# Two graph-attention layers and a binarised layer on one core: signs turned through DRAM, column maxima by halves, and work moved at the borders

## The chip, the core and the metric

The kernel runs on one core of a Trainium2 chip. The metric is the device time of one launch in microseconds, the median of several runs. Before the change it is 2627.36 us (three runs, 2627.24 to 2629.74). The engines' names are short here: PE is TensorE (PEld its weight loads), DVE is VectorE, ACT is ScalarE, POOL is GpSimd, SP is SyncE. SP issues nearly all loads, POOL most stores.

## The reference

```python
N, D = 3327, 512                       # x: N x D, adj: N x N of zeros and ones
def gat_layer(x, W, adj):              # W: D x 2D, twice (L = 2), with W_stack[0], W_stack[1]
    Wh, Ws = split(x @ W, 2, axis=-1)
    a = softmax(Wh @ Ws.T, axis=-1) * adj
    return leaky_relu(a @ Wh + x, 0.01)
h = layernorm(x + gat_layer(gat_layer(x, W[0], adj), W[1], adj))
xw = maximum(sign(h), 0) @ sign(weight).T
return layernorm(h + relu(adj @ xw))
```

All is float32 at the interface. The attention is dense, N x N scores for each of two layers; the last step multiplies adj by a matrix that comes from the signs of h.

## The kernel before, in words

**Tiles.** The N rows make NT = 26 tiles of P = 128 (the last one has 127 rows), 13 pairs of tiles (NQ = 13, a pair is called g on the query side, q on the key side) and 7 chunks of four tiles (NC = 7, the last one has two). Products of two-by-two blocks are made with seven multiplications instead of eight; the sums and differences of blocks that this needs are made by DVE, POOL or ACT, or ahead of time in DRAM (`xs_d`, `ws_d`, `gs_d`).

**Stages.** For each layer l, `project` (L297) turns x, makes the values `wh` and their block sums, the keys' block sums (`xs_d`) and the projected queries (`gs_d`). Then `attention` (L549) walks through 13 x 13 steps (g, q). After both layers, adj times xw is accumulated by `aggregate` (L1099), and `finale` (L1114) adds, normalises and writes out.

**A step of attention.** The loop over v (L985) writes out by hand what each step holds. `scores` for a later (chunk c, q, half s) run LOOK = 30 steps ahead of `values` of step v. In between, for steps v + 3 and v + 2: `shift` (L734, subtract the column's maximum), `exponential` (L738, ACT), `running` (L741, the running total), `masked` (L749, times adj), then `sums` (L785) on POOL, which builds the block sums `as` that PE's values product needs. Each piece of work carries a place within the step (0 to 1); the pieces of a step are sorted by it and put on their engines' queues in that order. An engine works through its queue in order. So the places decide what on DVE stands ahead of what. `halved_sums` (0.6), `halved` (0.61) and `exact` (0.62) make 8-bit block sums of adj for the last product, on DVE and ACT; `keep_blocks` stores them from POOL's queue one step later.

**Borders.** In the last step of a chunk's scores, `column_max` (L666) is put into the next step for both pairs of the chunk at once: fold the two rows of maxima (-0.04), turn and reduce and join the four partition groups (0.36), and turn back to `off` (0.9). The first maximum of a chunk is a copy (L648), the first total of a pair as well (L745). In a pair's last step, `take_out` (L827) reads the four accumulator banks of PSUM at 0.34, 0.63, 0.91 and 1.06; the next pair's products write into the same four banks.

**The end of a pair.** `finish` (L853) gives a list of small jobs (`later`), one for each following step, at place 0.7: `norm` (two PE transposes of the totals), `residual(i)` for both tiles (DVE, then a store by POOL), and in the second layer `sign(i)` (mean and comparison, DVE), `turn(i)` (L901: four PE transposes of 128 x 128 bf16 and one ACT copy) and `linear(i)` (four PE products with the sign of weight, then a store of xw or, for the last two pairs, a copy into its place in SBUF). There are 11 jobs for a pair in the second layer, and 9 for the last pair.

**Between the layers.** In the last steps of layer 0, `early` holds loads of the next weights, `turn_w` (DVE), `product_m` (PE, L281) and block sums. Then layer 1's `project` loads the first chunk of x1, transposes it by PE (L329 to L333, 16 transposes of f32, four ACT copies), and DVE makes the first two key sums (`left_sums`, L203).

Of the kernel before, what the change touches and what calls it, by code (L numbers as in the profile page):

```python
# [19 lines left out]
P = 128  # L20
# [10 lines left out]
def kernel(  # L31
# [18 lines left out]
    def rows(t):  # L50
        return min(P, N - t * P)
# [50 lines left out]
    h_d = tc.dram_tile([N, D], F32, name="h_d")  # L102
    xw_d = tc.dram_tile([NT, P, D], F16, name="xw_d")
# [122 lines left out]
    w_rows, w_laid, wT, m_of, wsum_of = {}, {}, {}, {}, {}  # L226
# [7 lines left out]
    def transpose_w(l, h, k, lane):  # L234
        pool, tag = lane
        pt = pool.tile([P, D], F32, tag=tag, name=f"pwT_{l}_{h}_{k}")
        for d in range(KD):
            nc.tensor.transpose(pt[:, ts(d, P)], w_rows[l, h, d][:, ts(k, P)], ident)
        wT[l, h, k] = slot([P, D], F32, f"wTs_{l}_{h}_{k}")
        copy_out(1 if h == 0 else k, wT[l, h, k], pt)  # L240
# [56 lines left out]
    def project(l, pre):  # L297
# [18 lines left out]
        def transpose_first(lane):  # L316

            pool, tag = lane
            xTs[0] = pre.tile([P, KD, CW], F32, tag="xT", bufs=2, name=f"xT_{l}_0")
            pts = [pool.tile([P, CW], F32, tag=tag, name=f"pxt_{l}_{k}") for k in range(KD)]  # L320
            xts = [t.rearrange("r (p k) -> r k p", k=KD) for t in rows_of[0]]
            if l == 0:

                for a in range(CT):
                    for k in range(KD):
                        nc.tensor.transpose(pts[k][:, ts(a, P)], xts[a][:, k], ident)
                for k in range(KD):
                    copy_out(k, xTs[0][:, k], pts[k])
                return  # L329
            for k in range(KD):  # L330
                for a in range(CT):
                    nc.tensor.transpose(pts[k][:, ts(a, P)], xts[a][:, k], ident)
                nc.scalar.copy(xTs[0][:, k], pts[k])  # L333

        def transpose_x(c, a):
            if a == 0:
                xTs[c] = pre.tile([P, KD, CW], F32, tag="xT", bufs=2, name=f"xT_{l}_{c}")
            nc.vector.transpose(
                xTs[c][:, :, ts(a, P)].rearrange("p k (r v) -> p r k v", v=B),
                rows_of[c][a].rearrange("p r (u k) -> p r k u", u=B),  # L340
            )


        load_x(0)
# [8 lines left out]
        transpose_first(acc_lane)  # L353
# [17 lines left out]
        def keys(c, a, between=lambda: None):  # L371

            q = c * CT // 2 + a
            xT = xTs[c]
            j1, j2 = ts(2 * a, P), ts(2 * a + 1, P)
            s12 = slot([P, 2, 2, P], F32, f"s12_{l}_{q}")
            s34 = slot([P, 2, 2, P], F32, f"s34_{l}_{q}")
            of = {
                A11: xT[:, 0:2, j1], A12: xT[:, 2:4, j1], A21: xT[:, 0:2, j2],
                A22: xT[:, 2:4, j2], S1: s12[:, 0], S2: s12[:, 1], S3: s34[:, 0],  # L380
                S4: s34[:, 1],
            }
            left_sums(
                *(of[i] for i in (A11, A12, A21, A22, S1, S2, S3, S4)), between=between
            )
            to = xs_d[l][q]
            for raw in (A11, A12, A21, A22):
                nc.gpsimd.dma_start(out=to[:, raw], in_=of[raw])
            nc.gpsimd.dma_start(out=to[:, S1 : S2 + 1], in_=s12)
            nc.gpsimd.dma_start(out=to[:, S3 : S4 + 1], in_=s34)  # L390
            return of
# [157 lines left out]
    def attention(l, att):  # L549
# [6 lines left out]
        asum, ws, out_ = {}, {}, {}  # L556
# [28 lines left out]
        def scores(c, q, s):  # L585
# [53 lines left out]
            def maximum(i):  # L639
                t = sc[i, q]  # L640
                if q == NQ - 1 and pad:
                    nc.vector.tensor_scalar(
                        t[:, 1], t[:, 1], there[:, 0:1], there[:, 1:2], ALU.mult, ALU.add
                    )
                if q == 0:
                    top[i] = att.tile([P, 2, HW], F32, tag=f"top{i % 2}", bufs=1,
                                      name=f"top_{l}_{i}")
                    nc.vector.tensor_copy(top[i], t)  # L648
                else:
                    nc.vector.tensor_tensor(top[i], top[i], t, ALU.max)  # L650

            if s == 1:

                after.append((-0.05, lambda: maximum(mine[0])))
                if q == NQ - 1:
                    after.extend(column_max(c))
# [9 lines left out]
        def column_max(c):  # L666

            mine = halves_of(c)
            n = len(mine) * HW // B


            part = small.tile([P, CW // B], F32, tag="mxq", bufs=1, name=f"mxq_{l}_{c}")
            quad = small.tile([P, P // B, CW // B], F32, tag="mx4", bufs=1,
                              name=f"mx4_{l}_{c}")
            whole = small.tile([P, CW // B], F32, tag="mx", bufs=1, name=f"mx_{l}_{c}")

            def fold():
                for g in mine:
                    nc.vector.tensor_tensor(
                        top[g][:, 0], top[g][:, 0], top[g][:, 1], ALU.max  # L680
                    )

            def across():
                w = HW // B
                for i, g in enumerate(mine):
                    nc.vector.transpose(top[g][:, 1], top[g][:, 0])
                    nc.vector.reduce_max(
                        part[:, ts(i, w)],
                        top[g][:, 1].rearrange("p (r u) -> p r u", u=B), axis=AX.X,
                    )  # L690
                for a in range(P // B):
                    nc.vector.tensor_copy(quad[:B, a, :n], part[ts(a, B), :n])
                nc.vector.reduce_max(
                    whole[:B, :n], quad[:B, :, :n].rearrange("p a r -> p r a"), axis=AX.X
                )
                for a in range(1, P // B):
                    nc.vector.tensor_copy(whole[ts(a, B), :n], whole[:B, :n])

            def back():
                w = HW // B  # L700
                for i, g in enumerate(mine):
                    off[g] = att.tile([P, 1, HW], F32, tag=f"off{i}", bufs=1,
                                      name=f"off_{l}_{g}")
                    nc.vector.transpose(
                        off[g][:, 0].rearrange("p (r u) -> p r u", u=B),
                        whole[:, ts(i, w)].unsqueeze(2).to_broadcast([P, w, B]),
                    )

            return [(-0.04, fold), (0.36, across), (0.9, back)]
# [28 lines left out]
        def exponential(g, q):  # L738
            nc.scalar.activation(sc[g, q], sc[g, q], AF.Exp)  # L739

        def running(g, q):  # L741

            if q == 0:
                total[g] = att.tile([P, 2, HW], F32, tag="total", name=f"total_{l}_{g}")
                nc.vector.tensor_copy(total[g], sc[g, q])  # L745
            else:
                nc.vector.tensor_tensor(total[g], total[g], sc[g, q], ALU.add)  # L747
# [53 lines left out]
        def values(g, q):  # L801
# [21 lines left out]
            if q == NQ - 1:  # L823
                got += [((i + 1.4) / 7, lambda i=i: take_out(g, i)) for i in (1, 3, 5, 6)]
# [28 lines left out]
        def finish(g):  # L853
# [37 lines left out]
            def sign(i):  # L891
# [7 lines left out]
                nc.vector.tensor_scalar(ba[:r], hh[:r], mv[:r, t, 0:1], None, ALU.is_gt)  # L899

            def turn(i):  # L901
                r = rows(mine[i])
                pt = ps_tr.tile([P, KD, P], BF16, tag="tr", name=f"pbt_{mine[i]}")
                for k in range(KD):
                    nc.tensor.transpose(pt[:, k, :r], held[i][:r, ts(k, P)], ident_h[:r, :r])
                held[i] = att.tile([P, KD, P], BF16, tag="baT", bufs=1, name=f"baT_{mine[i]}")
                nc.scalar.copy(held[i][:, :, :r], pt[:, :, :r])
# [18 lines left out]
            if not last:  # L926
                return [norm, lambda: residual(0), lambda: fetch(1), lambda: None,
                        lambda: residual(1)]
            free = [] if g == NQ - 1 else [lambda: None]
            return [  # L930
                norm, lambda: residual(0), lambda: (sign(0), fetch(1)), *free,
# [4 lines left out]
        if last:  # L936

            early, wts = {}, {}

            def load_weight(k):  # L940
                wts[k] = ring.tile([P, D], F32, tag="h", name=f"wT_{k}")
                nc.sync.dma_start(out=wts[k], in_=weightT[ts(k, P), :])
# [4 lines left out]
        else:  # L947

            end = len(ahead) - LOOK
            early, parts = {}, []  # L950
# [13 lines left out]
            n = len(steps) - end - 2  # L964
            early[end + 2] = [(0.2, begin_m)]
            for i, do in enumerate(product_m(l + 1, ch_lane)):
                early.setdefault(end + 2 + i * n // (KD * KD), []).append(
                    (0.3 + 0.4 * (i % 2), do)
                )
            early.setdefault(end + 7, []).append((0.6, lambda: parts.extend(sums_w(l + 1))))  # L970
            for i in range(4):
# [89 lines left out]
    def load_products(v):  # L1061
# [11 lines left out]
        for t in range(2 * NQ - 4):  # L1073
            g, i = divmod(t, 2)
            made = (g + 1) * NQ - 1 + (6, 11)[i]
# [38 lines left out]
    def finale(att):  # L1114
# [75 lines left out]

        constants()
        product_sums(NQ - 1)
# [143 lines left out]
```

## Time and profile before

| what | value |
|---|---|
| median of three runs | 2627.36 us |
| the profiled execution, its own time | 2626.88 us |
| its span, first to last instruction | 2625.1 us |
| granted TensorE clock, mean | 0.998 |
| DVE, ACT, POOL busy | 81%, 30%, 42% |
| DMA, mean rate | 243 GB/s |
| start of the first and the last step of attention's values, layer 0 | 279.0 and 1239.3 us |
| the same, layer 1 | 1500.9 and 2477.7 us |

The profile is one execution. Its page gives for each engine the time that it was busy, and groups of instructions by line and shape with the number, the busy time, the mean duration in ns, and the idle time before them with what ended it. The list of waits names an engine's line, what it waited for, the sum in us, how often, and the longest. The timeline lists instructions by start and length; a number in brackets is the idle time before, with the one that ended it. A table of stretches gives, for an engine, how long it was busy in each, with the granted clock and the share of the DMA engines' time. An engine that is named as the releaser may have been done long before; then it was another one.

### The profile page before, as it was taken

The numbers are of one execution on the slowest core, as the hardware profiler recorded it, in microseconds if no ns is written. First come the engines' busy times: TensorE is split into PE (matmuls) and PEld (weight loads), VectorE is DVE, ScalarE is ACT, GpSimd is POOL, SyncE is SP. The second block draws the span as 40 slices with busy tenths as digits, with TensorE's granted clock in tenths as the row PEclk, the third lists the DMA queues.
The fourth block names the chain that finished last, engine by engine and source line by source line (L and its number), as shares of the span: only waits on it lengthen the run. The fifth ranks groups of instructions, "written<-read, shape, count | busy, mean of one in ns | idle before, by whom it ended". The sixth has DMA issues, their size and how long they took to land. (4 is left out here: it accounts for less than half of the span.)

```text
span 2625.1 us, 40169 instructions
## 1 busy us (share of the span) xinstructions
PE 2582.4 (98%) x12552; PEld 2238.6 (85%) x12552; DVE 2116.0 (81%) x4376; ACT 785.9 (30%) x1954; POOL 1104.1 (42%) x2025
## 2 busy tenths in 40 slices
PE   9999999999999999999999999999999999999998
PEld 6888888888888888887888888888888888888787
DVE  6764888899898896777875689989899898767876
ACT  2323332333333332211332333333333333222143
POOL 3640344444444444546562144444444444455510
PEclk9999999999999999999999999999999999999999
DMA  6855777787777776787875668777787776688775
GB/s 209 296 193 180 240 242 269 232 276 249 263 245 246 267 241 223 236 254 245 284 243 179 226 223 283 250 242 265 238 283 245 236 271 233 226 263 264 260 249 171
DMA packets 308055, 639.16 MB, mean 243 GB/s; under 512 B 34855, under 2 KB 175745, under 8 KB 306298
## 3 DMA queue, kind: packets, MB, share of 16 engines
q1 hardware_dynamic: 272140, 530.29, 61.7%
q0 software_dynamic: 35664, 106.18, 11.0%
q8 instruction: 103, 1.69, 0.3%
q14 instruction: 118, 0.97, 0.1%
q10 hardware_dynamic: 30, 0.03, 0.0%
HBM read 529.69 MB, written 106.67 MB: 242 GB/s over the span
## 5 line engine op out<-in xcount | busy, mean ns | idle before, releaser
L580 PE MATMUL pZ<-gs,xs 128*128 128x256 f32 x2496 | 636.8, 379 | 2.0 <-ACT u L597 1.7
L790 POOL TENSOR_TENSOR as<-s 128x128 f32<-128x128 f32 x338 | 163.8, 485 | 1042.9 <-DVE s L752 888.2
L580 PEld LDWEIGHTS pZ<-gs,xs 128*128 128x128 f32 x2496 | 473.2, 190 | 69.2 <-ACT u L597 3.6
L817 PE MATMUL acc<-ws,s 128*128 128x256 f32 x1352 | 402.2, 379 | 0.0
L817 PE MATMUL acc<-wh,s 128*128 128x256 f32 x1352 | 355.7, 379 | 0.6 <-DVE s L752 0.4
L817 PE MATMUL acc<-ws,as 128*128 128x256 f32 x1352 | 348.0, 380 | 7.0 <-issue 4.0
L739 ACT ACTIVATE s<-s 128x512 f32<-128x512 f32 x338 | 213.4, 631 | 428.4 <-DVE s L736 428.3
L580 PE MATMUL pY<-gs,xs 128*128 128x256 f32 x1248 | 320.6, 379 | 1.7 <-ACT p L597 1.7
L817 PEld LDWEIGHTS acc<-ws,as 128*128 128x128 f32 x1352 | 255.9, 190 | 48.8 <-issue 8.9
L817 PEld LDWEIGHTS acc<-wh,s 128*128 128x128 f32 x1352 | 256.7, 190 | 36.2 <-DVE s L752 1.4
L817 PEld LDWEIGHTS acc<-ws,s 128*128 128x128 f32 x1352 | 256.0, 190 | 34.5
L650 DVE TENSOR_TENSOR top<-top,s 128x512 f32<-128x512 f32 x312 | 222.5, 726 | 73.1 <-ACT s L637 53.3
L580 PEld LDWEIGHTS pY<-gs,xs 128*128 128x128 f32 x1248 | 236.8, 190 | 35.0 <-ACT p L597 2.8
L736 DVE TENSOR_TENSOR s<-s,off 128x512 f32<-128x512 f32 x338 | 248.4, 735 | 0.1
L752 DVE TENSOR_TENSOR s<-s,adj 128x512 f32<-128x512 f32 x338 | 238.3, 705 | 8.9
L747 DVE TENSOR_TENSOR total<-total,s 128x512 f32<-128x512 f32 x312 | 232.5, 745 | 0.0
L792 POOL TENSOR_TENSOR as<-s 128x128 f32<-128x128 f32 x338 | 208.6, 617 | 26.5
L597 ACT COPY u<-pZ 128x256 f32<-128x256 f32 x312 | 115.7, 371 | 323.2 <-PE pZ L580 322.6
L817 PE MATMUL acc<-wh,as 128*128 128x256 f32 x676 | 202.5, 381 | 0.0
L791 POOL TENSOR_TENSOR s<-s 128x128 f32<-128x128 f32 x338 | 186.7, 552 | 27.4
L793 POOL TENSOR_TENSOR as<-s,as 128x128 f32<-128x128 f32 x338 | 181.8, 538 | 26.5
L622 DVE TENSOR_TENSOR s<-p,u 128x256 f32<-128x256 f32 x156 | 67.6, 433 | 139.0 <-ACT u L597 137.9
(218 smaller groups left out, 3864.0 us busy)
## 6 DMA issues: line engine op xcount, KB each, us to landing
ws<-ws_d SPq DMA_DIRECT2D x338, 512.0 KB, 3.8
xs<-xs_d SPq DMA_DIRECT2D x182, 512.0 KB, 5.9
adj<-in_adjT_dram SPq DMA_DIRECT2D x324, 256.0 KB, 4.3
xs<-xs_d SPq DMA_DIRECT2D x156, 384.0 KB, 6.4
gs_d<-gsp POOLq DMA_DIRECT2D x88, 256.0 KB, 3.0
gs<-gs_d SPq DMA_DIRECT2D x12, 1792.0 KB, 11.5
adj_d<-ab POOLq DMA_DIRECT2D x169, 112.0 KB, 3.9
ahl<-adj_d SPq DMA_DIRECT2D x78, 224.0 KB, 4.9
```

Source lines behind the costliest of these rows:

```text
L580: nc.tensor.matmul(ch[bank], xs[c, q, a][:, k], gs[c][:, b, k], start=(start and k == 0), stop=(k == 1), skip_group_check=True,)
L597: nc.scalar.copy(ch[name], ch[bank])
L650: nc.vector.tensor_tensor(top[i], top[i], t, ALU.max)
L736: nc.vector.tensor_tensor(s, s, off[g].to_broadcast([P, 2, HW]), ALU.subtract)
L739: nc.scalar.activation(sc[g, q], sc[g, q], AF.Exp)
L747: nc.vector.tensor_tensor(total[g], total[g], sc[g, q], ALU.add)
L752: nc.vector.tensor_tensor(s, s, adj[g, q], ALU.mult)
L790: nc.gpsimd.tensor_tensor(s3, a11, a21, ALU.subtract)
L791: nc.gpsimd.tensor_tensor(a21, a21, a22, ALU.add)
L792: nc.gpsimd.tensor_tensor(s2, a21, a11, ALU.subtract)
L793: nc.gpsimd.tensor_tensor(s4, a12, s2, ALU.subtract)
L817: nc.tensor.matmul(acc[g][i // 2][:, i % 2], a[i], b[i], start=(q == 0 and i % 2 == 0), stop=(q == NQ - 1), skip_group_check=True,)
```

## The change

It changes these things:

- **Signs.** For the first 11 of 13 pairs, the sign tile `ba` is stored to a DRAM tensor `ba_d` by POOL, loaded one step later by SP in four pieces of 32 partitions (`lay`, into the ring buffer that also holds xres and x0), and turned by DVE in blocks of 32 x 32 two steps after that. `fetch(1)` moves behind `turn(0)`. A pair has 13 jobs instead of 11. The last two pairs keep the PE transposes, with columns taken at a stride of four; weightT's rows are read in the matching order. The last but one pair's norm comes one step later.
- **Maxima.** `column_max` takes one pair. The first pair's four jobs (fold, turn, across, back) stand in the step after the chunk's last scores, the second pair's two, two, three and four steps after, at 0.68. The first maximum is taken of q = 0 and q = 1 together, and the copy falls away.
- **Totals.** For q = 0 ACT makes the exponential twice, once into the total; DVE's copy falls away.
- **take_out** of the second accumulator bank goes from 0.63 to 0.59.
- **Between the layers.** Layer 1's first chunk of x1 is loaded in pieces in steps 160 to 163, turned by DVE in steps 165 and 166 into a buffer of the `gs` ring, and its key sums are made in step 167; PE's transposes there fall away. `product_m` starts one step later. The copies of the turned weights in layer 0 are all ACT's.
- **The end.** `product_sums(NQ - 1)` is written ahead of `constants()`.

```diff
+    ba_d = tc.dram_tile([NT, P, D], BF16, name="ba_d")
...
-        copy_out(1 if h == 0 else k, wT[l, h, k], pt)
+        nc.scalar.copy(wT[l, h, k], pt)
...
-        load_x(0)
+        if l == 0:
+            load_x(0)
+        else:
+            xTs[0] = x_first[l]
...
-        transpose_first(acc_lane)
+        if l == 0:
+            transpose_first(acc_lane)
...
+            of = keys_first.pop((l, q), None) or key_sums(l, q, a, xTs[c], between)
...
-                if q == 0:
+                if q == 1:
...
-                    nc.vector.tensor_copy(top[i], t)
-                else:
+                    nc.vector.tensor_tensor(top[i], sc[i, 0], t, ALU.max)
+                elif q > 1:
...
-                    after.extend(column_max(c))
+
+                    after.extend(column_max(mine[0]))
+                    for i in mine[1:]:
+                        for n, (_, do) in zip((2, 2, 3, 4), column_max(i)):
+                            early.setdefault(v + n, []).append((0.68, do))
...
-            return [(-0.04, fold), (0.36, across), (0.9, back)]
+            return [(-0.04, fold), (0.2, turn), (0.5, across), (0.7, back)]
...
-            nc.scalar.activation(sc[g, q], sc[g, q], AF.Exp)
...
+                nc.scalar.activation(total[g], sc[g, q], AF.Exp)
+            nc.scalar.activation(sc[g, q], sc[g, q], AF.Exp)
...
-                nc.vector.tensor_copy(total[g], sc[g, q])
...
-                got += [((i + 1.4) / 7, lambda i=i: take_out(g, i)) for i in (1, 3, 5, 6)]
+                    for i, at in ((1, 0.34), (3, 0.59), (5, 0.91), (6, 1.06))
...
+                if g < NQ - 2:
+                    nc.gpsimd.dma_start(out=ba_d[t], in_=ba)
+
+            def lay(i):
+
+                bt = held[i] = ring.tile([P, P // B, P], BF16, tag="xr", name=f"bt_{mine[i]}")
+                load_laid(nc.sync, bt, ba_d[mine[i]], P)
...
+                    nc.vector.transpose(
+                        held[i].rearrange("p k (r v) -> p r k v", v=B),
+                        bt.rearrange("p r (u k) -> p r k u", u=B),
+                    )
...
+                return [
+                    norm, lambda: residual(0), lambda: sign(0), lambda: lay(0), lambda: None,
+                    lambda: (turn(0), fetch(1)), lambda: linear(0), lambda: residual(1),
+                    lambda: sign(1), lambda: lay(1), lambda: None, lambda: turn(1),
+                    lambda: linear(1),
+                ]
...
-            n = len(steps) - end - 2
+            n = len(steps) - end - 3
...
+                early.setdefault(n - 9 + a, []).append((0.9, lambda a=a: load_first(a)))
+                early.setdefault(n - 4 + a // 2, []).append((0.45, lambda a=a: turn_first(a)))
...
+                early.setdefault(n - 2, []).append((0.6 + a / 10, lambda a=a: keys_of_first(a)))
...
-            made = (g + 1) * NQ - 1 + (6, 11)[i]
+            made = (g + 1) * NQ - 1 + (7, 13)[i]
...
+        product_sums(NQ - 1)
         constants()
-        product_sums(NQ - 1)
```

## The prediction

> **What bounds the kernel now.** I read the page first, then TensorE's (PE's) waits, then the stretches where it waits. Lines are those of the kernel before. All durations are of the one profiled execution: span 2625.1 us, 2626.9 us with what lies around it, 0.5 us under the median of the three runs (2627.4).
>
> ```profile
> PE 2582.4 (98%) x12552; PEld 2238.6 (85%) x12552; DVE 2116.0 (81%) x4376; ACT 785.9 (30%) x1954; POOL 1104.1 (42%) x2025
> ```
>
> PE is busy in 98% of the span, 42.7 us are not. Some 11.8 us of these are the tail after the last matmul (2613.3 us), so only 31 us are gaps. A change can gain in two ways: fewer matmuls, or fewer gaps. The gaps, from PE's waits (us in total, times, longest):
>
> ```profile
> PE acc L817 <- issue: 4.0, 3, 1.7
> ...
> PE pX L580 <- DVE s L628: 3.5, 4, 1.2
> ...
> PE pz L865 <- POOL adj L716: 2.7, 1, 2.7
> PE pZ_wh L401 <- DVE s L205: 2.5, 1, 2.5
> PE pm L289 <- DVE wTs L260: 2.0, 1, 2.0
> PE agg L1109 <- DVE wh L212: 1.8, 1, 1.8
> ```
>
> Four of these are single waits at one place each, and the change moves the very work waited for. "Step" below is one (g, q) of attention, 6.1 us (g0 starts at 279.0, g1 at 358.0 us, 13 steps).
>
> **Signs through DRAM (22 of 26 tiles).** Removed: 22 x 4 PE transposes and 22 ScalarE copies (0.59 us each, ACT is 30% busy: nothing). What a tile's transposes take from PE, in the timeline:
>
> ```profile
> 1608.18 0.39 PE L905 MATMUL pbt<-ident_h,ba 128*128 128x128 bf16 x4
> 1608.41 0.65 PE L817 MATMUL acc<-wh,as 128*128 128x256 f32 x2
> 1608.89 0.59 PE L817 MATMUL acc<-ws,s 128*128 128x256 f32 x2
> ```
>
> The next matmul starts 0.23 us after them, and its pair takes 0.48 us from start to start where a pair takes 0.43: 0.28 us a tile, 22 x 0.28 = **6.2 us**. The Trainium skill speaks against the move ("VectorE: DVE Perf Modes", Rules for kernel authors: transpose 128x128 on TensorE if PSUM will do; The three transpose paths: 390 ns there, 311 ns on VectorE). At 390 ns each the gain would be 34 us; the row shows that transposes overlap, so I take 6.2.
>
> Added per tile: one POOL DMA issue (0.55 us, as its other stores), four SP DMA issues (0.43 us each), one VectorE (DVE) transpose. The nearest row for that:
>
> ```profile
> L338 DVE STREAM_TRANSPOSE xT<-xr 128x512 f32<-128x512 f32 x44 | 47.9, 1096 | 0.0
> ```
>
> Same element count and pattern, so 1.1 us; bf16 might be half (0.5), the skill's 4 x 311 ns would be 1.2. 22 x 1.1 = 24 us of DVE time, on the path only where DVE lags. DVE idles 0.5 to 3 us in most steps of layer 1, but hardly in the five steps after a chunk's border and in the last 15 steps. The turn of a pair's second tile comes now at q 11, two steps after the border, and residual and sign of that tile a step later, next to it. I charge **-1.0 us** (0 to -5: five borders at 1 us each).
>
> The new waits: on SP, the load waits for the store of the signs, and ws, adj and xs loads queue behind it. By its place (0.7 of the step) and its 1.4 us of work the sign ends about 1 us into the next step when DVE lags 3 us (an estimate); POOL's stores land after 4 us (xw_d 4.3), so SP is free before that step ends. The ws buffer it loads next is released only then, and is due two steps (12 us) later against 3.8 us to land: hidden, nothing. On POOL the store of the signs stands behind a step's block sums and ahead of the next step's, which PE needs two steps later: 0.55 us there, hidden. fetch(1) now waits for turn(0): due two steps later, 6 us to land, hidden. On DVE the turn waits for a load issued two steps earlier: hidden. Tile 21 alone falls into steps of 3 us; its risk is in the -5.
>
> **The border between the layers.** Removed: 16 f32 transposes of PE, from 1243.4 to 1245.3 us: **1.9 us**; and the key sums that PE waited for are now made in attention's last steps, where DVE is idle nearly whole steps (3.9 us at q 10 and 11). The wait and what follows:
>
> ```profile
> 1249.00:1251.40 2.40, 0.00 (x0) 1.00 0.68 205
> 1251.40:1254.90 3.50, 3.48 (x9) 0.54 0.96 305
> ```
>
> (stretch, its length, PE busy, granted clock.) After the 2.46 us gap the clock is halved for 3.4 us, so the gap costs 2.46 + 1.7 = **4.2 us**. The skill ("TensorE: Matmul & The Clock Gate", Why this matters for your kernels) asks only for gaps under about 3 us; by it the gap would cost 2.5. The row decides: 4.2 (from 1.5, if DVE, which would then be about 2 us nearer to PE, makes it wait at chunk 1). wa was issued at 1233.6 and takes 5.5 us; PE needs it at 1243.3: hidden. The four more SP issues in each of four 3.9 us steps (1.7 us beside 0.8) fit.
>
> The projection product starts a step later, after its DVE turns: the 2.0 us wait goes: **2.0** (1.0 to 2.0). wT's copies on ACT: the 1.16 us gap at 17.4 us waited for a DVE copy: **0.5** (0 to 1.2).
>
> **Take-outs and maxima.** Where a pair g begins, PE waits for the second accumulator bank to be read:
>
> ```profile
> 598.90 0.69 DVE L650 TENSOR_TENSOR top<-top,s 128x512 f32<-128x512 f32 x1
> 599.50 0.42 DVE L843 TENSOR_TENSOR ou<-acc,op 128x256 f32<-128x256 f32 x1
> 599.96 0.42 DVE L844 TENSOR_TENSOR ou<-acc,ou 128x256 f32<-128x256 f32 x1
> ```
> ```profile
> 600.48 0.89 PE L817 MATMUL acc<-ws,as 128*128 128x256 f32 x3 [1.56 <-issue]
> ```
>
> The profile calls it "issue", but PE starts when L844 has read the bank. At 0.59 this read stands ahead of the block sums (0.6), the exact check and the maximum: some 3 us sooner. Such gaps: 1.56, 1.70, 0.72 (598.9, 917.7, 1987.8 us), in all 4.0; I take **3.0** (1.5 to 4.0), since DVE is then further behind.
>
> The maxima by halves: before, a border costs DVE fold 0.8 + across 3.2 + back 0.8 = 4.7 us in one step, plus 0.8 for two first copies and 0.4 to 0.5 for the total's. After: 0.4 + 0.9 + 1.4 + 0.4 = 3.1 us for each half, 6.1 over four steps, since the small copies (0.16 us) come twice. The sum is the same, only flatter. It should remove the pX gaps (1.2 at 425.4, 0.7 at 745.3), but DVE is busy 39.8 of 41 us from 415 to 456 us, and the following gap (1.2 at 457.8, 0.45 at 777.4) comes when DVE's work and a store behind it are done. So PE arrives earlier and waits longer: **0** (0 to 3). Rows of weightT in another order and xw loads that follow their later stores are the same bytes: nothing. The second exponential costs ACT 26 x 0.63 us, a step ahead of its reader: nothing.
>
> **The end.** product_sums ahead of the constants, which wait 1.3 us for an activation table: **1.8 us** (1.0 to 1.8). Pair 11's norm a step later: the 2.7 us wait goes, but the last steps are DVE's:
>
> ```profile
> 2424.00:2432.00 8.00, 7.69 (x15) 1.00 0.95 314
> 2432.00:2436.00 4.00, 2.44 (x5) 1.00 0.91 335
> 2436.00:2476.00 40.00, 38.44 (x74) 1.00 0.87 301
> ```
>
> (third number: DVE busy.) DVE idles only because it waited for that same product (1.5 us), so only this comes back: **1.5** (0 to 2.7).
>
> **Sum.** 6.2 + 1.9 + 4.2 + 2.0 + 0.5 + 3.0 + 1.8 + 1.5 - 1.0 = 20.1 us. 2626.9 - 20.1 = 2606.8 of the profiled execution, 2607.3 as a median. All ends at their best give 27, at their worst 8 us: 2600 to 2619.
>
> **Rivals.**
> - *Gaps only move* (DVE paces the borders and the end, as it already does at 415 to 456 us): only the removed matmuls (8.1), product_sums (1.8), the product's wait (2.0) and the bare border gap count, 12 to 14 us: 2614. For it: DVE at 96% in these stretches. Against: at the border of the layers DVE is idle.
> - *The profile's gaps go entirely*, the pX and end ones too: 27 us, 2600. For it: flatter DVE work. Against: the same sums.
> - *Slower: SP is held by the signs' round trip.* If the store lands more than 5 us into the step of the load, ws and xs come late and PE stops, 22 times. Gone are 20 us at 0.9 us a tile; at 1.6 us a tile the sum is 35 and the time 2642. For it: DMA engines 70 to 80% busy, ACT already waited 20 us for adj_d stores. Against: two steps' reserve, and PE waits for a DMA only 1.2 us in all of attention.
> - *No change*: this needs half that price, 0.9 us a tile.
>
> **Chances.** Forecast 0.60, gaps move 0.24, all gaps go 0.08, no change 0.04, slower 0.04. 0.2% (5.3 us) is about what a measurement of this kernel can tell: faster 0.92, same 0.04, slower 0.04. The range goes from all gaps gone to a little beyond "gaps move": 2600 to 2618.
>
> **What would show it.** PE matmuls fewer by 104 transposes (their records), PE busy down by 8 to 10 us; no wait of pZ_wh on L205's successor, full clock at the border; no 1.6 us gaps at 599 and 918 us; pm, agg and pz gone from the waits. Wrong: new PE waits on ws or xs DMAs, DVE transposes of bt over 1.5 us, gaps in layer 1's steps 0 to 5 after a border above 5 us in sum, or longer gaps at 458 and in the last 15 steps.

## The result and the profile after

The changed kernel takes 2621.64 us (median of 19 runs, 2617.40 to 2626.44), the kernel before in the same measurement 2627.24 us (19 runs, 2623.97 to 2630.91). The ratio is 0.9979, 95% interval [0.9972, 0.9986]: 5.6 us faster. The prediction said 2607.3 us, 2600 to 2618; the gain is a quarter of it. Its profiled execution has a span of 2619.8 us and a granted clock of 0.998. The page's row of engines:

```profile
PE 2579.2 (98%) x12423; PEld 2232.0 (85%) x12448; DVE 2114.9 (81%) x4444; ACT 786.8 (30%) x1956; POOL 1098.2 (42%) x2047
```

PE has 104 transposes less to do (104 weight loads fewer, 12552 before) and is busy 3.2 us less, where 8 to 10 were foreseen (with three buffers, run 1 below, it is 8.5). The idle times of PE up to its last matmul add up to 30.5 us; they were 31.0 before. So the waits named in the prediction went, and others took their place. PE's waits now (us in total, times, longest):

```profile
PE pY L587 <- ACT p L604: 7.1, 5, 2.0
PE pZ L587 <- ACT u L604: 4.7, 6, 1.3
PE acc L821 <- POOL as L796: 4.7, 7, 1.2
...
PE pX L587 <- DVE s L635: 1.4, 2, 0.7
PE acc L821 <- DVE h L856: 1.3, 2, 0.7
PE pz L872 <- POOL adj L720: 0.9, 1, 0.9
```

pm, agg and pZ_wh are gone from the list, and pz fell from 2.7 to 0.9, as foreseen. The waits of pY and pZ for ScalarE have grown. Before, they were:

```profile
PE pZ L580 <- ACT u L597: 1.7, 2, 1.1
PE pY L580 <- ACT p L597: 1.7, 2, 1.2
```

Steps are counted from 0 in each layer. The start of each step, set beside the same step before, says where time is lost: 5.5 us from step 25 to 30 of layer 0, 4.4 us from step 77 to 82 (the two borders of chunks there). In layer 1 a lead of 3.2 us at step 0 falls to 0.8 us at step 156, although 22 tiles x 0.28 us of transposes came off on the way.

What pY waits for stands in the timeline of ACT and DVE at step 25 of layer 0 (start, length, engine and line; the bracket is the idle time before):

```profile
433.14 0.40 ACT L762 CAST ab<-adj 128x256 fp8e4<-128x256 f32 x1 [3.03 <-DMA adj_d<-ab]
433.14 0.29 DVE L776 TENSOR_TENSOR ab<-adj 128x128 fp8e4<-128x128 f32 x1 [3.02 <-DMA adj_d<-ab]
...
433.65 0.36 ACT L604 COPY p<-pY 128x256 f32<-128x256 f32 x1
```
```profile
434.06 1.13 PE L587 MATMUL pY<-gs,xs 128*128 128x256 f32 x4 [1.48 <-ACT p L604]
```

The halved blocks `ab` of adj have two buffers. ACT and DVE stand 3.0 us until an earlier store of blocks has landed (issued by POOL at 426.8, 6.3 us before) and its buffer is free. Behind the waiting cast, in ACT's queue, is the copy of a score product, and PE needs that bank back. The same happens at step 29 (2.04 us of PE), 77 (1.65) and 81 (1.80); at 29 and 81 the timeline names the store for DVE alone, and ACT's cast starts within 0.05 us of DVE's block sum. The waits of ACT and DVE for this store over the whole kernel, before and after:

```profile
ACT ab L758 <- DMA adj_d<-ab: 20.4, 13, 5.4
...
DVE ab L772 <- DMA adj_d<-ab: 17.3, 14, 4.2
```
```profile
ACT ab L762 <- DMA adj_d<-ab: 34.1, 16, 5.0
...
DVE ab L776 <- DMA adj_d<-ab: 30.2, 16, 3.8
```

The gap of 2.04 us also halves the clock, as the 2.46 us at the layers' border did before (stretch, length, PE busy, clock):

```profile
457.00:460.00 3.00, 2.41 (x11) 1.00 0.94 341
460.00:464.00 4.00, 1.96 (x7) 0.84 0.61 230
464.00:468.00 4.00, 4.00 (x16) 0.73 0.27 66
```

Ahead of the last matmul, each kernel's trace has one such half-clock stretch of 3.41 us: it has only moved from the border of the layers to step 29, at 1.7 us in both places.

The small copies of the maxima are the second sign. Groups by shape, before and after (busy us, mean ns):

```profile
L692 DVE COPY mx<-mxq 32x16 f32<-32x16 f32 x48 | 7.8, 163 | 0.9
L697 DVE COPY mx<-mx 32x16 f32<-32x16 f32 x36 | 6.0, 166 | 0.7
```
```profile
L698 DVE COPY mx<-mxq 32x8 f32<-32x8 f32 x104 | 23.7, 228 | 1.1
L703 DVE COPY mx<-mx 32x8 f32<-32x8 f32 x78 | 17.9, 230 | 1.6
```

They move half as many elements and take 0.23 us instead of 0.16; with the few 32x8 ones of before, 41.6 us instead of 16.1, or 1.8 us more at each of 14 borders. In the changed kernel's trace 110 of these 182 copies run while POOL works on a sum; they take 0.27 us in the mean. The other 72 take 0.16.

### The profile page after: what moved, and what is told of

Its sections match the earlier page's. It is cut to its first block, busy times and chain, and to the rows that moved or that the text cites. A ratio compares the mean times of both kernels' runs of the same rounds, so it can differ in the third digit from the quotient of the medians.

```text
span 2619.8 us, 40057 instructions
## 1 busy us (share of the span) xinstructions
PE 2579.2 (98%) x12423; PEld 2232.0 (85%) x12448; DVE 2114.9 (81%) x4444; ACT 786.8 (30%) x1956; POOL 1098.2 (42%) x2047
## 5 line engine op out<-in xcount | busy, mean ns | idle before, releaser
L794 POOL TENSOR_TENSOR as<-s 128x128 f32<-128x128 f32 x338 | 162.3, 480 | 1013.8 <-DVE s L756 824.2
L657 DVE TENSOR_TENSOR top<-top,s 128x512 f32<-128x512 f32 x286 | 200.1, 712 | 77.5 <-ACT s L644 51.8
L796 POOL TENSOR_TENSOR as<-s 128x128 f32<-128x128 f32 x338 | 199.4, 590 | 26.5
```

What stands on the lines that cost most here:

```text
L794: nc.gpsimd.tensor_tensor(s3, a11, a21, ALU.subtract)
L796: nc.gpsimd.tensor_tensor(s2, a21, a11, ALU.subtract)
```

## The experiments

Three theories for the missing 14 us: **S**, the blocks' store with two buffers, which is worse where DVE and ACT come earlier and find more behind it; **C**, the maxima by halves are simply dearer; **D**, the turns of the signs put DVE behind in layer 1. Times are medians of 4 to 10 runs; the kernel before stood at 2626.8 to 2628.1 us beside them. The intervals of the ratios are about 3.5 us wide to each side for 4 to 6 runs, so a difference of 2 or 3 us between two variants needs the traces beside it. Profiled executions with the same code ahead of attention reach its step 0 at 276.4 to 280.2 us; what a change does to a stage is therefore taken from that stage's first step on.

**1. Three buffers for the blocks.**

```diff
-                [P, 7, P], F8, tag="adj_b", bufs=2, name=f"ab_{l}_{g}_{q}"
+                [P, 7, P], F8, tag="adj_b", bufs=3, name=f"ab_{l}_{g}_{q}"
...
-                held[i] = att.tile([P, KD, P], BF16, tag="baT", bufs=1, name=f"baT_{mine[i]}")
+                held[i] = att.tile([P, KD, P], BF16, tag="ba", bufs=1, name=f"baT_{mine[i]}")
```

> The changed kernel, with three buffers in place of two for the halved adjacency blocks (they wait in SBUF for their store to DRAM), and the turned signs in the same buffer as the signs. Theory S (at the chunk borders of layer 0 VectorE and ScalarE now run into the store of these blocks and stand still for 2.4 to 3.0 us, twice a border, and the four gaps of TensorE at 432.6, 460.1, 755.4 and 783.0 us, 7.0 us together, come from that): 4 to 7 us faster than the changed kernel's 2621.6 us, these gaps under 0.5 us each. Theory C (VectorE has simply more work there, the maxima by halves with their small copies): the wait for the store goes, the gaps stay, within 1.5 us of 2621.6.

Measured: 2609.34 us (0.9933 of before [0.9919, 0.9946]), 12.3 us faster than the changed kernel, more than S asked. The list of waits no longer has adj_d for DVE or ACT, and none of the four gaps is over 0.1 us. In the profiled executions the last matmul comes 15.4 us sooner than in the changed kernel: 2.3 us of it before step 0 of layer 0, 12.5 in layer 0, 0.6 after that. (The second part of the edit touches only the signs of layer 1, so the gain in layer 0 is the third buffer's.) DVE's busy time in the stretch after the first border, in the changed kernel and with three buffers:

```profile
431.00:461.00 30.00, 24.85 (x60) 1.00 0.74 233
```
```profile
431.00:461.00 30.00, 29.32 (x63) 1.00 0.78 251
```

So at the border, where there is most to do, DVE stood still for 5 us of 30; with a third buffer for 0.7. A gap costs more than its length: the steps with these gaps are longer by another 0.27 us each, and the half clock costs 1.7.

**2. Maxima of both halves at once** (`column_max` and its call as before; two buffers).

```diff
-                    after.extend(column_max(mine[0]))
-                    for i in mine[1:]:
-                        for n, (_, do) in zip((2, 2, 3, 4), column_max(i)):
-                            early.setdefault(v + n, []).append((0.68, do))
+                    after.extend(column_max(c))
```

> The changed kernel, with the column maxima again for both halves at once, in the step after the last scores, as in the kernel before (the first maximum and the second exponential stay as changed). Theory C (a pair of halves costs VectorE 6.7 to 7.4 us against 4.7 before, since the small copies come twice and, beside GpSimd's sums, take 0.23 us and not 0.16): 3 to 6 us faster than 2621.6, and layer 1 gains back most of the 8.5 us that went missing there. Theory S: the old gap ahead of pX (1.2 us) returns, and the time is 1 to 4 us longer. The prediction's own reading (the same sum, only flatter) gives 0 to 3 us longer.

Measured: 2611.02 us (0.9938 [0.9924, 0.9951]), 10.6 us faster than the changed kernel. C's sign was right, but not its place: in the profiled executions 9.7 us are gained in layer 0, where PE's gaps fall from 10.8 to 5.2 us, 1.4 are lost between the layers, and 2.4 gained in layer 1, where C had foreseen most of 8.5. DVE still waits 28.2 us for the store. The gaps ahead of pX that the halves were to remove do return (0.93 and 0.75 us in layer 0; 1.71 twice in layer 1, where the kernel before has none) and cost less than the halves.

**3. All signs turned by PE** (`ba_d`, `lay` and the DVE turn left out, steps as before; two buffers).

```diff
-                if g < NQ - 2:
-                    nc.gpsimd.dma_start(out=ba_d[t], in_=ba)
...
-                    norm, lambda: residual(0), lambda: sign(0), lambda: lay(0), lambda: None,
-                    lambda: (turn(0), fetch(1)), lambda: linear(0), lambda: residual(1),
-                    lambda: sign(1), lambda: lay(1), lambda: None, lambda: turn(1),
-                    lambda: linear(1),
...
                 *(free if g == NQ - 2 else []), norm, lambda: residual(0), lambda: (sign(0), fetch(1)), *free,
                 lambda: turn(0), lambda: linear(0), lambda: residual(1), lambda: sign(1), *free,
                 lambda: turn(1), lambda: linear(1),
```

The list that served the last two pairs now serves all.

> The changed kernel, with the signs of all 26 tiles again turned by TensorE and copied by ScalarE, without the round trip through DRAM, at the steps of the kernel before. If the signs' part is worth what its own terms say (6.2 less 1.0 us): 5 us slower than 2621.6, 2626 to 2627. Theory D (the turns and the late steps at the borders push VectorE behind, and TensorE waits in layer 1 for most of what it saved): 0 to 2 us slower. Theory C (layer 1 loses to the maxima, not to the turns): 5 us slower again.

Measured: 2619.46 us (0.9968 [0.9956, 0.998]): 2.2 us *faster* than with the signs through DRAM, though every step with a turn on PE is 0.28 us longer, as worked out. PE's gaps in layer 1 fall from 13.5 to 6.5 us; those at steps 24, 26, 76 and 78 are gone. That is beyond all three expectations; D comes nearest. By the medians alone it is hardly clear of noise, but from the first to the last step of layer 1 the traces give 2.5 us as well.

**4. The small copies ahead of POOL's sums.**

```diff
-            return [(-0.04, fold), (0.2, turn), (0.5, across), (0.7, back)]
+            return [(-0.04, fold), (0.1, turn), (0.36, across), (0.7, back)]
...
-                            early.setdefault(v + n, []).append((0.68, do))
+                            early.setdefault(v + n, []).append((0.36 if n == 3 else 0.68, do))
```

> The changed kernel, with the small copies of the maxima at 0.36 of the step, for both halves, and the turn of the first half at 0.1: ahead of the masking and so ahead of GpSimd's sums. Theory C in its narrow form (what is dear is that the copies run beside GpSimd, 0.23 us mean and up to 0.46, in place of 0.16): the copies fall to about 0.16 us, 1.6 us of VectorE at each chunk border, and the kernel is 2 to 4 us faster than 2621.6. If the place of the copies does not matter, or if they hold up the masking instead: within 1.5 us.

Measured: 2618.51 us (0.9969 [0.9956, 0.9981]), 3.1 us faster. The groups:

```profile
L698 DVE COPY mx<-mxq 32x8 f32<-32x8 f32 x104 | 18.0, 173 | 1.6
L703 DVE COPY mx<-mx 32x8 f32<-32x8 f32 x78 | 12.6, 162 | 1.6
```

The copies are back at the old duration: it was POOL beside them that stretched them. That is some 3 of the 10.6 us, by the medians; in the profiled executions layer 0 gains 4.8 us (1.7 of them the half clock, which is gone), and layer 1 loses 4.5, of which 2.4 is a wait for a load of xs at step 136. (The gap of 1.10 us at step 52, which the take-out at 0.59 had closed, came back.)

**5. Neither part**: 2 and 3 together.

> The changed kernel without its two large parts: the column maxima of both halves at once and all signs turned by TensorE, both as before; the border of the layers, the take-outs, the second exponential, the first maximum and the end stay as changed. The prediction's terms for what is left are 1.9 + 4.2 + 2.0 + 0.5 + 3.0 + 1.8 + 1.5 = 14.9 us: 2612 to 2613. If the two parts, undone one at a time (10.6 and 2.2 us), simply add up: 2608 to 2610. If the signs only lose where the maxima by halves are in the way: 2614 to 2617.

Measured: 2609.41 us (0.9932 [0.9918, 0.9945]). The parts add up: 2621.6 less 10.6 and 2.2 is 2608.8. Against the kernel before the last matmul is 14.9 us sooner, the very sum of the prediction's remaining terms. That the sum agrees to the tenth is partly luck: ahead of attention 1.4 us are gained where the term was 0.5, in layer 0 2.4 for some 4.5, between the layers 6.0 for 6.1, in layer 1 3.2 for some 2, after it 1.9 for 1.8. Another 1.7 us come from the stretch after the last matmul, and lie behind the issue of the last store. This stretch is 11.6 to 12.0 us in the three kernels without the second exponential (before, runs 6 and 12), and 10.0 to 10.3 in all others; why, was not looked into.

**6. The kernel before with three buffers** (edit 1 on the kernel before).

> The kernel before, with three buffers in place of two for the halved adjacency blocks and the turned signs in the buffer of the signs. Theory S (the wait for the store became costly only through the change, since there the maxima stand in steps in which VectorE used to catch up): 0 to 3 us faster than 2627.7, at most the gaps of 1.2 and 0.45 us at 457.8 and 777.4 us go. Rival (two buffers were short all along, whatever the change): 8 to 12 us faster.

Measured: 2620.79 us (0.9976 [0.9967, 0.9986]), 6.0 us faster than before, between S and its rival. Two buffers were short all along, at about 6 us; the third buffer is worth 5.5 (maxima whole, signs by PE: 2609.4 to 2603.9, run 10), 6.6 (maxima whole: 2611.0 to 2604.4, run 9) and 12 to 14.5 us (halves: runs 1 and 8). So it is the halves that double the price of the store. With three buffers on both sides the change brings 11.5 us, not 5.6.

**7 and 8. Three buffers, and the second tile's signs, or all signs, turned by PE** (8 is edits 1 and 3 together; this is 7, in `sign` and `turn`).

```diff
-                if g < NQ - 2:
+                if g < NQ - 2 and i == 0:
...
-                    lambda: sign(1), lambda: lay(1), lambda: None, lambda: turn(1),
+                    lambda: sign(1), lambda: None, lambda: turn(1),
```

> The changed kernel with three buffers for the blocks, and of each pair of tiles only the first tile's signs through DRAM and VectorE, the second tile's turned by TensorE a step sooner, as before. Theory D (what the signs lose in layer 1 is the second turn, which falls two steps after each border): costs 11 transposes at 0.28 us (3.1), gains the gaps of 0.7 and 0.6 us at steps 24, 26, 76 and 78 and half of the two of 1.3 us, with what each gap costs beside its own length 4 to 6 us: 1 to 3 us faster than the 2609.3 us of three buffers alone. Rival (the first tile's turn and its late fetch hold VectorE up): the gaps stay, 2611 to 2613.

> The changed kernel with three buffers for the blocks and all signs turned by TensorE as before. If the two effects are apart in time (the blocks in layer 0, the signs in layer 1): 2.2 us faster than three buffers alone, 2606 to 2608. If the turns only lost because VectorE was behind by the store as well: 2613 to 2615, as the 22 x 0.28 us come back.

Measured: 2606.58 and 2604.97 us, 2.8 and 4.4 us faster than run 1. With all signs on PE, the gaps at steps 24, 26, 76 and 78 are gone. With the second tile's alone, those at 26 and 78 are gone, and those at 24 and 76 fall from 0.70 to 0.42 us. Apart from the store, then, the signs through DRAM lose 4.4 us by the medians, and 2.3 in the traces' layer 1.

**9 and 10. Three buffers and whole maxima, with signs through DRAM (edits 1 and 2) or by PE (1, 2 and 3).**

> The changed kernel with three buffers for the blocks and the column maxima of both halves at once, as before. If the maxima by halves cost only through the wait for the store (10.6 us with two buffers): the same as three buffers alone, 2608 to 2611. If they also cost by their own work: 2604 to 2607. If, with the store out of the way, they are worth what flatter work should bring (no gaps of 0.8 to 1.7 us ahead of pX at steps 24 and 76): slower, 2612 to 2616.

> The changed kernel with three buffers for the blocks, the column maxima of both halves at once and all signs turned by TensorE. Against the 2605.0 us with the maxima by halves it weighs the halves alone with neither the store nor the turns in their way: if they gain the pX gaps (1.2 us, twice in layer 0, with their surcharge 0.3 each), 2607 to 2609; if they are only dearer work, 2601 to 2604; if neither, within 1.5 us of 2605.

Measured: 2604.39 and 2603.92 us. With three buffers the halves cost 4.9 us beside the turns and 1.1 us without them. So of their 10.6 us beside the turns, about half was paid through the store; of the 10.1 us without the turns (run 3 less run 5), nearly all.

**11. Idle turns**: run 3 with 22 more transposes of 128x512 bf16 on DVE in layer 1, at the changed kernel's steps, into a tile that nobody reads.

```diff
+            if last and 0 <= v < NQ * (NQ - 1) and v >= NQ and v % NQ in (5, 11):
+                work += [(0.7, twin)]
```

> The kernel in which TensorE turns all signs (two buffers, 2619.5 us), with 22 idle turns added on VectorE in layer 1: a strided transpose of 128x512 bf16 that nobody reads, at the steps of the changed kernel's turns (5 and 11 of each pair), and nothing on the DMA queues. Theory D (VectorE's turn itself puts TensorE off at the borders): the gaps at steps 24, 26, 76 and 78 of layer 1 come back, 3 to 6 us slower than 2619.5. Rival (the round trip's place in the order, the stores on GpSimd's queue or the late residual put it off): within 1.5 us of 2619.5.

Measured: 2618.26 us, 1.2 us below run 3; in the traces, layer 1 takes 0.7 us longer than in run 3, and one gap of 0.45 us (step 78) is back. So the turn's own cost does not explain the loss: 22 x 0.7 us of DVE, with residual and sign at their early steps, cost 0.7 us at most. D in this form is refuted.

**12. One exponential**: run 8 with DVE's copy into the total in place of ACT's second exponential.

```diff
-                nc.scalar.activation(total[g], sc[g, q], AF.Exp)
...
+                nc.vector.tensor_copy(total[g], sc[g, q])
```

> The kernel of three buffers with all signs turned by TensorE (2605.0 us), with the first step's sums copied by VectorE as before, in place of the second exponential on ScalarE. The prediction gave the second exponential nothing; VectorE gets 26 copies of 0.4 us back, one at the start of each pair. If VectorE's time there counts: 1 to 3 us slower. If the second exponential holds up ScalarE's copies of the products (gaps ahead of pY and pZ by ScalarE, 0.57 us at steps 54 and 106): 1 to 2 us faster. Else within 1 us.

Measured: 2610.69 us, 5.7 us slower than run 8. In the profiled executions the last matmul is 4.6 us later: 2.0 of it before step 0 of layer 0, where kernels with the same code differ by as much, 2.0 in layer 0 (steps 0, 28, 80 and 104), and 0.6 in step 0 of layer 1. The stretch after the last matmul is 2.0 us longer, too. So the second exponential is worth 2.6 us in attention, and with that stretch, if it belongs to it, 4.6.

**13 and 14. The second tile one step sooner, or later.** What the idle turns of run 11 had not moved was the place of the second tile's residual and sign. Run 13 is run 1 without the empty step ahead of `turn(0)`; run 14 is run 8 with an empty step ahead of `residual(1)`, and no round trip.

```diff
-                    norm, lambda: residual(0), lambda: sign(0), lambda: lay(0), lambda: None,
+                    norm, lambda: residual(0), lambda: sign(0), lambda: lay(0),
                     lambda: (turn(0), fetch(1)), lambda: linear(0), lambda: residual(1),
...
-                lambda: turn(0), lambda: linear(0), lambda: residual(1), lambda: sign(1), *free,
+                lambda: turn(0), lambda: linear(0), *free, lambda: residual(1), lambda: sign(1), *free,
```

> The changed kernel with three buffers for the blocks, all 22 tiles still through DRAM, but without the empty step between the load of the signs and the first turn: the second tile's residual, sign and turn come one step sooner (6, 7 and 10 of the pair). Theory E (the second tile's residual and sign, 2.1 and 1.4 us of VectorE, come one step too late: VectorE idles 2.5 us at step 20 and is 2 us later at the border): VectorE's lag at step 22 falls from 6.2 to 4.3 us, the gaps at steps 24, 26, 76 and 78 go, 3 to 5 us faster than three buffers alone (2609.3): 2604 to 2606. Rival (the round trip's stores and loads put it off): within 1.5 us of 2609.3.

> The kernel of three buffers with all signs turned by TensorE (2605.0 us), and an empty step ahead of the second tile's residual, so that its residual and sign come at 7 and 8 of the pair, as in the changed kernel, with no round trip. Theory E: the lag at step 22 rises to about 6.2 us and gaps come back at the steps after the borders, 2 to 5 us slower, 2607 to 2610. Rival: within 1.5 us of 2605.0.

Measured: 2602.17 us, 7.2 us faster than run 1 (in the traces, layer 1 is 6.7 us shorter); and 2608.43 us, 3.5 us slower than run 8. DVE's stretches in steps 20 to 23 of layer 1, run 1 and then run 13 (busy us, of the step's length):

```profile
1605.78:1612.25 6.47, 3.96 (x10) 1.00 1.05 395
1612.25:1617.86 5.61, 5.44 (x12) 1.00 0.79 302
1617.86:1624.68 6.82, 6.61 (x16) 1.00 0.90 289
1624.68:1630.30 5.62, 5.28 (x19) 1.00 0.40 115
```
```profile
1608.98:1615.45 6.47, 6.23 (x15) 1.00 1.00 392
1615.45:1621.06 5.61, 5.47 (x13) 1.00 0.95 359
1621.06:1627.54 6.48, 6.27 (x16) 1.00 0.67 188
1627.54:1633.15 5.61, 5.34 (x16) 1.00 0.91 318
```

In run 1 DVE idles 2.5 us in step 20, two steps ahead of the border, because the residual is queued at the end of that step, behind work that waits for PE (1.3 us) and for ACT (1.1 us). In run 13 that room is used. The mask product queued in step 22 then starts 4.3 us into the step instead of 6.2, and the gaps at 24, 26, 76 and 78 go; those at 54 and 106 fall from 1.34 to 0.57 us. In run 14 it starts at 6.2, in run 8 at 4.3.

But the late step is not the whole cause. Run 14 brings back only the gaps at 24 and 76, at 0.42 us, and so does run 7, where residual and sign are late and the second turn is PE's. PE's wait there in run 1, and then in runs 7 and 14, which have the same line:

```profile
PE pX L587 <- DVE s L635: 1.4, 2, 0.7
```
```profile
PE pX L587 <- DVE s L635: 0.8, 2, 0.4
```

The longer gaps at 24 and 76, with those of 0.6 to 0.7 us at 26 and 78, need both the late residual and, behind it, DVE's turn of the same tile (in run 1 it starts 8.8 us after PE begins step 24, in run 13 1.5 us after it). Of run 14's 3.5 us, 1.2 arose before layer 1, where the code is the same, and the two gaps with what they cost beside their length make 1.4. So in the traces the late residual and sign alone cost 2.3 us (run 14 against run 8, from layer 1 on), the idle turns alone at most 0.7 (run 11), and the two together 6.7 (run 1 against run 13).

**15. Run 13 with whole maxima.**

> Three buffers, maxima of both halves at once, all signs through DRAM with the empty step taken out: the joined kernel. Theory E: the gaps of 1.7 us ahead of pX at steps 24 and 76 of layer 1 shrink as well, 2 to 4 us faster than the 2604.4 us of the same kernel with the empty step: 2600 to 2602.5. If these gaps belong to the whole maxima: within 1.5 us of 2604.4.

Measured: 2602.66 us, the same as run 13, and 1.7 us faster than run 9; the gaps at steps 24 and 76 fall from 1.71 to 0.74 us. With the store and the step mended, it no longer matters which maxima are used. Runs 13 and 15, at 0.9905 of before (run 13: [0.9889, 0.992]), are the fastest kernels here, and run 13 has the whole of the change in it.

## Why the prediction was wrong, point by point

- **Border of the layers, 1.9 + 4.2**: right. In run 5, from the last step of layer 0 to the first of layer 1, 6.0 us are gained, and the clock is full there.
- **Product's wait 2.0, wT's copies 0.5, take-outs 3.0, product_sums 1.8, the end 1.5**: right in kind. The product's 2.0 are 1.5 net, since pz now waits 0.9 at step 156; the gap at wT fell from 1.16 to 0.68; steps 52 and 104 gained 1.35 and 1.63; agg's 1.8 is gone; the last 13 steps gained 0.9 of 1.5, and PE waits there for POOL's sums in other places. That run 5 measured just the 14.9 us of these terms and the border is partly luck, as said there.
- **Signs, 6.2 - 1.0**: the 0.28 us a tile are there. The row for the turn was a good bound (0.70 us, in the range 0.5 to 1.2), and the loads land 1.9 us after issue. But the round trip through SP was not wholly hidden. At step 133 SP stands until the store of the signs has landed, 5.1 us after its issue in run 1; the load of xs comes out behind it, and PE waits 1.2 us for xs at step 136. This wait, 0.25 to 2.4 us long, stands in all eight traces with signs through DRAM and in none of the nine others. So the rival "slower" had its mechanism at one place of 22. **The term -1.0 (0 to -5) failed**, by size: the working named the place, "residual and sign of that tile a step later, next to" the border, but charged 1.0 us for all of it, and 1 us a border at the worst. By the difference to the signs on PE it is 8.4 us (6.2 + 2.2), and 3.4 us in run 13. What was not asked is which step had room: the late residual leaves a hole of 2.5 us, then meets the border, and the late turn comes on top of it.
- **Maxima by halves, 0 (0 to 3)**: **this step failed.** They cost 10.6 us. Two things stood behind the 0. "The sum is the same": it took 0.16 us for a copy from rows where POOL was idle, and most of the new places lie beside POOL's sums, which makes the mean 0.23. That is about 3 us of the time (run 4). The other thing is the store: with a third buffer 5.7 of the 10.6 us go (runs 1 and 9), and with the second tile a step sooner as well, the halves cost nothing (runs 13 and 15). The prediction saw "a store behind it" in the gap at 457.8, and among its rivals even that ACT waits 20 us for these stores. But it took this as a sign of busy DMA engines; it did not ask what stands behind that wait in ACT's queue, nor whether the wait would grow. Its sign of being wrong, "longer gaps at 458", came: 1.2 became 2.04 us.
- **The second exponential, "nothing"**: right as a cost, but what it spares DVE was left out. It gains 2.6 us or more (run 12).
- The rival *gaps only move* (2614) was the right mechanism at the wrong place and too small: the border of the layers and the take-outs kept their gain, and the new waits, those that came with the halves and with the signs, cost some 12 us (2621.6 less the 2609.4 of run 5).

What stays open: why exactly the halves make the store's wait twice as dear. That they do is shown by runs 1 to 3, 5, 6 and 8 to 10. That the second half's across and back now stand in the queue behind the waiting block sums, where the whole maxima were done ahead of them, is seen in the order, but was not tried alone. The 1.7 us after the last matmul and PE's seven waits for POOL's sums at the very end are open too.

## What to carry to other kernels

When work is moved so that an engine arrives sooner, look for the next wait in its queue that does not move with it, here a store with two buffers, and ask what is queued behind that wait on *each* engine that takes part. A job that is put one step later costs not its own length but the idle room that it leaves and the crowded step that it enters: read the busy time of the engine per step before choosing the step. A duration from a row holds for the neighbours of that row.

## What the runs showed of the hardware

- Up to the last matmul, every half-clock stretch in these traces is 3.41 us long, and the full-clock stretches between are whole multiples of it (450.56 us is 132 of them, 1242.45 us is 364), so the clock seems to be judged in fixed windows. The length of a gap alone does not decide. Gaps of 2.04, 2.41, 2.46 and 2.98 us halved the clock; those of 2.36 us (run 4) and 2.51 us (run 11) did not; gaps of 2.01 and 2.69 us in the kernel before did not, and at the same places in run 6 did. What decides is how much of a gap falls into one window. Laid on the grid of 3.41 us that starts with a trace's first full-clock stretch, the idle time of PE in the window before is 2.01 to 2.46 us in all seven cases of half clock in the 17 traces, and in no other window is it above 1.85 us: the gap of 2.69 us in the kernel before lay across two windows. So here the limit lies between 1.85 and 2.01 us of idle time in a window of 3.41, and where a gap falls in it is chance. The Trainium skill ("TensorE: Matmul & The Clock Gate", Part 1) speaks of a free-running window of about 3.4 us, but puts the loss of clock after at least one idle window; here six tenths of one were enough.
- A copy of 32x8 f32 on DVE takes 0.16 us alone and 0.27 us in the mean (up to 0.46) while POOL works on a sum.
- A DVE transpose of 128x512 in 32x32 blocks takes 0.70 us in bf16 and 1.10 us in f32.
- A gap of PE costs mostly 0.27 us on top of its length, even where the clock stays full: set beside the same step of layer 0 in kernels without the gap, a step is longer by that at gaps of 0.45 to 2.5 us (steps 25, 29, 77 and 81 in seven kernels; elsewhere in layer 0 it was 0.2 to 0.3, and nothing at step 104).
